# A two-layer graph attention network on one core: three pairs' attention, the second layer's bias additions and sums, and the last group's scaling put elsewhere in the order

## Chip, cores and metric

The kernel runs on one core of one Trainium2 chip. The metric is device time in microseconds (us) of one execution. TensorE (PE), VectorE (DVE), ScalarE (ACT), GpSimd (POOL) and SyncE (SP, which issues the DMAs here) each work through their instructions in the order in which the program lists them; waits between engines go by semaphores.

## The reference

128 graphs of 64 nodes with 768 features, fp32. Each of two layers is followed by a residual addition and a layer norm; x goes in, the output of the second norm comes out.

```python
# layer 0: gated graph attention, 12 heads of 64
h = einsum('bnd,ade->bane', x, W);  th = tanh(h)
attn = (th . w_src) + transpose(th . w_dst)
attn = softmax(where(~adj, -999, leaky_relu(attn, 0.2)))
f = elu(einsum('banm,bame->bane', attn, h) + b)       # heads side by side
gate = sigmoid(x @ H_w.T + H_b)
x = layernorm(x + gate * f + (1 - gate) * x)
# layer 1: masked self-attention, 6 heads of 128
q, k, v = x @ Wq + bq, x @ Wk + bk, x @ Wv + bv
p = softmax(q k^T / sqrt(128) + where(adj, 0, NEG))
x = layernorm(x + (p v) @ Wf + bf)
```

## The kernel before, in words

Two graphs make a tile of 128 rows; there are 64 tiles. `phase_a` (L304 to 773) does layer 0 and the value product of layer 1, for 32 pairs of tiles. `phase_b` (L776 to 1146) does the rest of layer 1 for 16 groups of two pairs.

*Dense products.* In phase A a product of a pair with a 768x768 matrix is done in a Strassen-like way with seven partial products instead of eight, each a step of three fp32 matmuls (`Product`, L196 to 250; the trace holds two matmul records for each, all at L208). It needs four sums of blocks of the transposed tokens, made on GpSimd by four instructions (`token_sums`, L254 to 260; "sums" below). The first partial product goes into a PSUM tile X; ScalarE copies it out (`snap`, L404), and the third partial product is added onto X, so the third cannot start before the first's snap is done. In phase B a similar scheme has R = 15 steps (`STEPS`, L37 to 53) that need 11 sums (`SUMS`, `SUM_STEPS`); those for F, the output product, are made on GpSimd by `pair_sum` (L842 to 846).

*The order.* Nothing schedules at run time or build time: each function is registered for a step in a table (`at`), and the steps are run through in order, functions of one step in the order of their registration (`run`, L262). With dense products as the clock of the table, this fixes every engine's queue. Pair p of phase A begins at o = 21 p: seven steps of W (h), seven of G (the gate), and seven of a value product V (`start_v`, L439 to 449). V belongs to an earlier pair: pair p's runs at o + 56, in pair p + 2. So pairs 0 and 1 have no V behind their G, nor has pair NP-2 = 30, whose seven steps are left free because pair 28's V was put into the last pair; the steps o + 14 to o + 20 of these three pairs hold no dense product.

*Attention of a tile in layer 0* (class `Tile0`, L455 to 623), with the steps that it has from its own start s (s = o for tile 1, which is first, o + 5 for tile 0, in the last pair o + 3): tanh of h; products with w_dst and w_src (`dst_mul`, `src_mul` on GpSimd, L467, L475) and their sums per head on VectorE (L470, L479); `dst_out` and `dst_in` send the dst scores to HBM and back, spread over the rows, as the tile s; `add` (L515, GpSimd adds src, then Prelu on ScalarE, L518); `mask` and `top` on VectorE (L522, L526); `exp`, twelve activations on ScalarE (L531); `scale`, a reciprocal and a multiplication on GpSimd for each half (L539, L541); `probs`, transposes on PE, copied by ScalarE (L552, L557); `aggregate` on PE (L570); `elu`, `mix1`, `mix2`; the layer norm, partly on GpSimd (`norm1`, L290 to 298: pow and shift) and with the normalisation on ScalarE (L302); `spill` to HBM. `gate_in` (L580, GpSimd) adds the gate's bias and `gate` (L584, ScalarE) takes its tanh.

For pairs 0 and 1 everything from `exp` on is two steps later for both tiles (`slow`), and tile 1's exps are kept in the table `late` and put at the end of their step, behind what the next pair registers there. The transposes of a pair's tokens and their sums stand at o - 6 to o - 4, for pairs 1, 2 and 31 by 7, 5 and 4 steps (`lead`) earlier.

*Phase B.* A group takes 90 steps: q and k for two halves, and in steps 60 to 89 the two F products (q = 0, 1 in the code) of the group before; the last group does its own F there. `load_x` fetches the residual rows, `add_bf` (L818 to 821) adds F's bias to them on GpSimd, two instructions for each q. The softmax of a group runs in tiles (q, i): in the last group maximum (`sm_top`), six exps on ScalarE (`sm_top_exp`, L952), and `sm_scale` (L968 to 971), a reciprocal on VectorE and one multiplication of 128x384 on GpSimd, then `probs` (L977, copied at L983) and `context` (L997).

The excerpt that shows how the order of the second F's sums is fixed before (f is the first step of that F):

```python
t = max(f - R + max(SUM_STEPS[: k + 1]) + 1, pr + 10)
at(t, lambda d=d, q=q, k=k: pair_sum(d, q, k))
```

Of the kernel before, what the change touches and what calls it, by code (L numbers as in the profile page):

```python
# [9 lines left out]
F32 = mybir.dt.float32  # L10
# [51 lines left out]
def kernel(  # L62
# [242 lines left out]
    def phase_a(ctx):  # L305
# [324 lines left out]
        late = {}  # L630

# [20 lines left out]
        for p in range(NP):  # L652
# [11 lines left out]
            if p:  # L664
                at(o - 20, lambda d=d: xb_in(d, 0))
                at(o - 16, lambda d=d: xb_in(d, 1))

                lead = {1: 7, 2: 5, NP - 1: 4}.get(p, 0)
                at(o - 6 - lead, lambda d=d: xT(d, 0))
                at(o - 5 - lead, lambda d=d: xT(d, 1))  # L670
                at(o - 4 - lead, lambda d=d: sums(d))
            else:
                at(0, lambda d=d: d.update(T=[transposed(t) for t in d["x"]]))
                at(0, lambda d=d: sums(d))
# [5 lines left out]


            slow = 2 if p < 2 else 0
            for i, s in ((1, o), (0, o + (5 if p < NP - 1 else 3))):
                t = Tile0(p, i)
                at(s + 6 + (i == 0), t.tanh, t.cap)
                at(s + 7, t.dst_mul)
                at(s + 8, t.src_mul)
                at(s + 9, t.dst_sum, t.dst_out, t.exchange)
                at(s + 10, t.src_sum)
                at(s + 13, t.dst_in)  # L690
                at(o + (14 if i else 16), t.gate_in)
# [12 lines left out]
                at(z + 24, t.probs)  # L704
                at(z + 25, t.aggregate)
                at(z + 26, t.elu)
                at(z + 27, t.mix1)
                at(z + 28, t.mix2)
                at(z + 29, t.norm1)
                at(z + 30, t.norm2)  # L710
                at(z + 31, t.spill)
# [58 lines left out]
        for step, fs in late.items():  # L770
            events.setdefault(step, []).extend(fs)
# [4 lines left out]
    def phase_b(ctx, wq, wk):  # L776
# [282 lines left out]
        for g in range(NG):  # L1059
# [35 lines left out]
            for q in range(2):  # L1095
                f = o + ((6 if last else 10) + q) * R
                for i in range(2):
# [88 lines left out]
```

## Time and profile before

| | us |
|---|---|
| median of three runs | 2965.62 |
| lowest, highest | 2964.14, 2966.01 |
| the profiled execution, as timed | 2965.09 |
| span of the profile | 2963.0 |
| VectorE busy | 1812.2 |
| GpSimd busy | 1642.1 |
| ScalarE busy | 1063.3 |

The profile is of one execution. Its page gives the busy time of each engine, the span in 40 slices, the chain of work that ended last and the costliest groups of instructions. Views of the trace list each engine's waits with what ended them, and its instructions in order of time; a line of such a timeline has start and length in us, the engine, the line of the code, the operation, output and inputs with shape, the number of instructions that the line stands for, and in brackets the idle time before and what ended it. Idle time matters on the engine that bounds the kernel, and there it is read stage by stage.

### The profile page before, as it was taken

The page shows a single profiled execution, that of the slowest core. Times are in us where ns is not written, and L with a number is a line of the kernel's source. Part 1 is how long each engine was busy: PE and PEld are TensorE (multiplying, and loading weights), DVE is VectorE, ACT ScalarE, POOL GpSimd, SP SyncE. Part 2 cuts the span into 40 slices and gives each one's busy share as a digit, 9 for nine tenths or more (in the row PEclk, how much of TensorE's full clock was granted, in tenths as well). Part 3 has the DMA queues.
Part 4 walks back from the last instruction along what each step waited for, and adds up shares of the span by engine and source line. Part 5 has one row for each costly group of instructions (what it writes and reads, how often), then busy time and mean ns, then how long its engine had stood idle before and what let it go on. Part 6 is the DMA issues. An engine that isn't in the chain of part 4 may idle for free.

```text
span 2963.0 us, 50040 instructions
## 1 busy us (share of the span) xinstructions
PE 2847.2 (96%) x18108; PEld 2063.0 (70%) x18108; DVE 1812.2 (61%) x3710; ACT 1063.3 (36%) x3011; POOL 1642.1 (55%) x1709
## 2 busy tenths in 40 slices
PE   7799999999999999999779999999999999999997
PEld 4455555555555555555448888888888888888886
DVE  4667667667677676676564555555555555555555
ACT  3354555545545545545432112222211222221222
POOL 3666666665665666665563544455454455455445
PEclk9899999999999999999899999999999999999999
DMA  6243443444544534534361112122212212211222
GB/s 183 84 143 114 133 146 113 144 132 123 148 122 133 148 114 133 149 114 136 112 197 40 56 64 87 55 86 87 74 56 76 87 55 87 87 66 62 78 81 70
DMA packets 358966, 309.13 MB, mean 104 GB/s; under 512 B 226625, under 2 KB 304193, under 8 KB 358721
## 3 DMA queue, kind: packets, MB, share of 16 engines
q1 hardware_dynamic: 358720, 305.95, 34.1%
q8 instruction: 144, 2.36, 0.3%
q14 instruction: 102, 0.83, 0.1%
HBM read 192.19 MB, written 101.06 MB: 99 GB/s over the span
## 4 chain that ended last, share of the span: by engine, by line
PE 60%; DVE 14%; POOL 10%; ACT 8%; DMA 5%; issue 3%; SPq 1%; POOLq 0%; DVEq 0%; ACTq 0%
PE X L863 42%; PE X L208 12%; ACT s L531 5%; POOL gt L580 3%; DMA xT_d<-T 2%; DVE s L522 2%; PE pb L997 2%; PE pb L928 2%; POOL s L541 2%; DVE nmx L526 1%; POOL th L475 1%; DVE pt L611 1%; DMA s<-dst_d 1%; DVE pt L602 1%; DVE pt L603 1%
## 5 line engine op out<-in xcount | busy, mean ns | idle before, releaser
L208 PE MATMUL X<-w,S 128*128 128x384 f32 x2304 | 804.1, 495 | 61.5 <-ACT snap L404 55.9
L208 PEld LDWEIGHTS X<-w,S 128*128 128x128 f32 x2304 | 431.8, 192 | 361.3 <-issue 59.0
L863 PE MATMUL X<-S,w 128*128 128x256 f32 x2816 | 668.0, 382 | 5.0 <-DVE q L889 2.4
L208 PE MATMUL X<-w,T 128*128 128x384 f32 x1728 | 598.5, 489 | 4.6 <-ACT snap L404 3.0
L863 PEld LDWEIGHTS X<-S,w 128*128 128x128 f32 x2816 | 523.2, 190 | 82.5 <-POOL shift L298 5.7
L208 PEld LDWEIGHTS X<-w,T 128*128 128x128 f32 x1728 | 327.9, 192 | 226.9 <-ACT snap L404 3.6
L845 POOL TENSOR_TENSOR Sc<-cT 128x256 f32<-128x256 f32 x224 | 160.8, 727 | 378.3 <-PE X L863 376.2
L863 PE MATMUL X<-w,Sc 128*128 128x256 f32 x1408 | 325.6, 383 | 1.9 <-DVE xs L906 1.9
L906 DVE TENSOR_TENSOR xs<-xs,X 128x256 f32<-128x256 f32 x512 | 208.5, 419 | 185.2 <-PE X L863 154.8
L863 PEld LDWEIGHTS X<-w,Sc 128*128 128x128 f32 x1408 | 264.5, 191 | 44.1 <-DVE xs L906 9.0
L531 ACT ACTIVATE s<-s,nmx 128x64 f32<-128x64 f32 x768 | 256.1, 336 | 93.3 <-DVE nmx L526 93.3
L889 DVE TENSOR_TENSOR k<-k,X 128x256 f32<-128x256 f32 x320 | 133.6, 421 | 217.8 <-PE X L863 167.9
L541 POOL TENSOR_TENSOR s<-s,rs 128x384 f32<-128x384 f32 x128 | 125.6, 981 | 220.4 <-DVE rs L539 156.0
L889 DVE TENSOR_TENSOR q<-q,X 128x256 f32<-128x256 f32 x320 | 132.2, 420 | 188.6 <-PE X L863 131.1
L863 PE MATMUL X<-xb,w 128*128 128x256 f32 x960 | 236.7, 379 | 0.0
L302 ACT ACTIVATE xs<-xs,shift,rstd 128x768 f32<-128x768 f32 x62 | 63.5, 1024 | 470.2 <-POOL shift L298 451.3
L404 ACT COPY snap<-X 128x384 f32<-128x384 f32 x288 | 136.1, 473 | 244.1 <-PE X L208 244.0
L467 POOL TENSOR_TENSOR tmp<-th,wd_bc 128x768 f32<-128x768 f32 x64 | 136.9, 2139 | 131.5 <-ACT th L463 131.5
L884 ACT ACTIVATE k<-X,bk_c 128x256 f32<-128x256 f32 x192 | 91.0, 474 | 305.2 <-PE X L863 305.2
L863 PEld LDWEIGHTS X<-xb,w 128*128 128x128 f32 x960 | 181.4, 190 | 23.8
L971 POOL TENSOR_TENSOR s<-s,rs 128x384 f32<-128x384 f32 x64 | 53.0, 828 | 227.6 <-DVE rs L970 204.7
L833 POOL TENSOR_TENSOR S<-xb 128x512 f32<-128x512 f32 x103 | 130.7, 1282 | 84.1 <-DMA xb<-xT_d 57.2
(109 smaller groups left out, 4072.9 us busy)
## 6 DMA issues: line engine op xcount, KB each, us to landing
xb<-in_x_dram SPq DMA_DIRECT2D x64, 384.0 KB
s<-dst_d SPq DMA_DIRECT2D x128, 192.0 KB
x_d<-xb SPq DMA_DIRECT2D x64, 384.0 KB
xT_d<-T SPq DMA_DIRECT2D x64, 384.0 KB
v_d<-v SPq DMA_DIRECT2D x128, 192.0 KB
xb<-xT_d SPq DMA_DIRECT2D x32, 768.0 KB
xb<-v_d SPq DMA_DIRECT2D x256, 96.0 KB
xs<-x_d SPq DMA_DIRECT2D x64, 384.0 KB
```

What stands on the lines that cost most here:

```text
L208: nc.tensor.matmul(o, self.lhsT(i, c), rhs, start=first and c == 0, stop=last and c == CH - 1, skip_group_check=True,)
L404: nc.scalar.copy(t, ps)
L467: nc.gpsimd.tensor_tensor(self.tmp, self.th, wd_bc, ALU.mult)
L531: nc.scalar.activation(self.s[:, a], self.s[:, a], AF.Exp, bias=self.nmx[:, a : a + 1], accum_out=self.sm[:, a : a + 1],)
L541: nc.gpsimd.tensor_tensor(t, t, rs[:, :, None].to_broadcast([P, A // 2, S]), ALU.mult)
L580: nc.gpsimd.tensor_tensor(self.g, self.g, hb_bc, ALU.add)
L833: eng.tensor_tensor(t, group_part(d, r0), group_part(d, r1), op)
L845: nc.gpsimd.tensor_tensor(t, pair_part(d, q, r0), pair_part(d, q, r1), op)
L863: nc.tensor.matmul(ps, self.lhsT(r, slot, c), self.rhs(r, slot, c), start=start and c == 0, stop=stop and c == 1, skip_group_check=True,)
L884: nc.scalar.activation(o[:, b], ps, AF.Identity, bias=bias[:, hd : hd + 1], scale=1.0 if positive else -1.0)
L889: nc.vector.tensor_tensor(o[:, b], o[:, b], ps, ALU.add if positive else ALU.subtract)
L906: nc.vector.tensor_tensor(o, o, ps, ALU.add if positive else ALU.subtract)
```

## The change

1. In phase A, for tile 1 of the pairs 0, 1 and 30: `dst_in` at s + 12 (was s + 13), `add` at s + 14 (was s + 17), mask and maximum at s + 15, exps at s + 16, scaling at s + 18 and s + 19. What follows from `probs` on is at s + 24 and on for all pairs; for pairs 0 and 1 it was two steps later, for both tiles. The table `late` is gone.
2. The token sums of pairs 1, 2 and 31 are at o - 4, as for the other pairs; the transposes keep their lead.
3. In the last pair tile 0 starts at o + 5 like in the others, its transposes for layer 1 are two steps later, and so are the pair's sums and its value product.
4. In phase B the second F's sums go each to one step behind its need (no longer behind all sums listed before it), or to that of the sums that it is made of; counted from f - R, the steps of the 11 sums go from 1, 2, 10, 10, 10, 10, 10, 10, 11, 12, 13 to 1, 2, 10, 10, 5, 9, 9, 8, 11, 12, 13. The bias additions are at f - 8 instead of f - 5, but for the last group.
5. In the last group the scaling is a reciprocal on VectorE and six activations on ScalarE of 128x64, each with its head's reciprocal as scale, in the place of one GpSimd multiplication; transposes and context are one step later, and so are F's sums.

```diff
-                lead = {1: 7, 2: 5, NP - 1: 4}.get(p, 0)
...
-                at(o - 4 - lead, lambda d=d: sums(d))
+                at(o - 4, lambda d=d: sums(d))
...
-            slow = 2 if p < 2 else 0
-            for i, s in ((1, o), (0, o + (5 if p < NP - 1 else 3))):
+            for i, s in ((1, o), (0, o + 5)):
...
-                at(s + 13, t.dst_in)
+                z = s - 3 if i and (p < 2 or p == NP - 2) else s
+                at(s + 12 if z < s else s + 13, t.dst_in)
+                at(z + 17, t.add)
                 at(o + (14 if i else 16), t.gate_in)
                 at(o + (16 if i else 18), t.gate)
-                at(s + 17, t.add)
-                at(s + 18, t.mask, t.top)
-                z = s + slow
-                if slow and i:
-                    late.setdefault(z + 19, []).extend((lambda t=t: t.exp(0), lambda t=t: t.exp(1)))
-                else:
-                    at(z + 19, lambda t=t: t.exp(0))
-                    at(z + (19 if i else 20), lambda t=t: t.exp(1))
+                at(z + 18, t.mask, t.top)
+                at(z + 19, lambda t=t: t.exp(0))
+                at(z + (19 if i else 20), lambda t=t: t.exp(1))
                 at(z + 21, lambda t=t: t.scale(0))
                 at(z + 22, lambda t=t: t.scale(1))
-                at(z + 24, t.probs)
+                at(s + 24, t.probs)
...
-                    at(o + 41 - i, lambda d=d, i=i: x1T(d, i, transposed(d["x"][i])))
+                    at(o + 43 - i, lambda d=d, i=i: x1T(d, i, transposed(d["x"][i])))
...
-                at(o + (47 if p < NP - 1 else 42), lambda d=d: x1_sums(d))
-            v = o + {NP - 4: 84, NP - 2: 50, NP - 1: 43}.get(p, 56)
+                at(o + (47 if p < NP - 1 else 44), lambda d=d: x1_sums(d))
+            v = o + {NP - 4: 84, NP - 2: 50, NP - 1: 45}.get(p, 56)
...
+        def sm_scale_act(d, q, i):
+            s, rs = sm_part(d, q, i), small.tile([P, HEADS], F32, name="rs1")
+            nc.vector.reciprocal(rs, d["sm", q, i])
+            for h in range(HEADS):
+                nc.scalar.activation(s[:, h], s[:, h], AF.Identity, scale=rs[:, h : h + 1])
...
-                        at(t + 5, lambda d=d, q=q, i=i: sm_scale(d, q, i))
-                        at(t + 7, lambda d=d, q=q, i=i: probs(d, q, i))
-                        at(t + 10, lambda d=d, q=q, i=i: context(d, q, i))
+                        at(t + 5, lambda d=d, q=q, i=i: sm_scale_act(d, q, i))
+                        at(t + 8, lambda d=d, q=q, i=i: probs(d, q, i))
+                        at(t + 11, lambda d=d, q=q, i=i: context(d, q, i))
...
-                pr = sm + (5 + 13 * q if last else 8 + 8 * q)
+                pr = sm + (6 + 13 * q if last else 8 + 8 * q)
+                ready = {}
...
-                        t = max(f - R + max(SUM_STEPS[: k + 1]) + 1, pr + 10)
+                        t = max(
+                            [f - R + SUM_STEPS[k] + 1, pr + 10]
+                            + [ready[r] for r in SUMS[k][:2] if r in ready]
+                        )
+                        ready[6 + k] = t
...
-                at(f - (1 if last else 5), lambda d=d, q=q: add_bf(d, q))
+                at(f - (1 if last else 8), lambda d=d, q=q: add_bf(d, q))
```

More of the change, by code (lines that the diff above doesn't have):

```diff
@@ L628, in at @@
             events.setdefault(max(step, 0), []).extend(fs)
-        late = {}
         def dense(d, key, i):
@@ L689, in phase_a @@
                 at(s + 10, t.src_sum)
-                at(s + 13, t.dst_in)
+                z = s - 3 if i and (p < 2 or p == NP - 2) else s
+                at(s + 12 if z < s else s + 13, t.dst_in)
+                at(z + 17, t.add)
                 at(o + (14 if i else 16), t.gate_in)
                 at(o + (16 if i else 18), t.gate)
-                at(s + 17, t.add)
-                at(s + 18, t.mask, t.top)
-                z = s + slow
-                if slow and i:
-                    late.setdefault(z + 19, []).extend((lambda t=t: t.exp(0), lambda t=t: t.exp(1)))
-                else:
-                    at(z + 19, lambda t=t: t.exp(0))
-                    at(z + (19 if i else 20), lambda t=t: t.exp(1))
+                at(z + 18, t.mask, t.top)
+                at(z + 19, lambda t=t: t.exp(0))
+                at(z + (19 if i else 20), lambda t=t: t.exp(1))
                 at(z + 21, lambda t=t: t.scale(0))
                 at(z + 22, lambda t=t: t.scale(1))
-                at(z + 24, t.probs)
[L705 to L711, printed above, removed]
+                at(s + 24, t.probs)
+                at(s + 25, t.aggregate)
+                at(s + 26, t.elu)
+                at(s + 27, t.mix1)
+                at(s + 28, t.mix2)
+                at(s + 29, t.norm1)
+                at(s + 30, t.norm2)
+                at(s + 31, t.spill)
             def x1_in(d, i):
@@ L769, in phase_a @@
         at(o + 30, lambda: load_T4(0))
-        for step, fs in late.items():
-            events.setdefault(step, []).extend(fs)
         run(events, N * NP + 60)
```

## The prediction

> **What bounds the kernel now.** The page comes first, for the engines' shares and the slices.
>
> ```profile
> PE 2847.2 (96%) x18108; PEld 2063.0 (70%) x18108; DVE 1812.2 (61%) x3710; ACT 1063.3 (36%) x3011; POOL 1642.1 (55%) x1709
> ...
> PE   7799999999999999999779999999999999999997
> ```
>
> TensorE (PE) is busy 96% of 2963.0 us: all that scheduling can win is its idle time, 2963.0 - 2847.2 = 115.8 us, plus matmuls that run slowly after a gap. The change removes no matmul. A slice is 74 us: the 7s are slices 1 and 2 (pairs 0 to 2), 20 and 21 (end of the first layer), and the last. Next, the waits of PE, for who ends its idle time (us in total, times, longest):
>
> ```profile
> PE X L208 <- ACT snap L404: 58.9, 33, 18.2
> PE pa L570 <- ACT pt L557: 10.0, 3, 7.3
> ...
> PE pb L977 <- POOL s L971: 6.8, 2, 6.1
> ```
>
> Half of it is one wait: the third product of a stage adds onto PSUM tile X, so it needs ScalarE's copy of X (the snap). The timeline of PE tells where (start, length, row, in brackets idle before and releaser):
>
> ```profile
> 59.50 8.72 PE L208 MATMUL X<-w,S 128*128 128x384 f32 x18 [6.90 <-ACT snap L404]
> ...
> 112.46 5.91 PE L208 MATMUL X<-w,S 128*128 128x384 f32 x12 [17.04 <-ACT snap L404]
> ...
> 1436.86 3.96 PE L208 MATMUL X<-w,S 128*128 128x384 f32 x6 [18.21 <-ACT snap L404]
> ...
> 1487.56 5.80 PE L208 MATMUL X<-w,S 128*128 128x384 f32 x12 [4.08 <-ACT snap L404]
> ...
> 2904.00 0.90 PE L977 MATMUL pb<-ident,s 128*128 128x128 f32 x3 [6.06 <-POOL s L971]
> ```
>
> So 42 us lie at three borders of pairs (0|1, 1|2, 30|31), just those where no value product follows the gate product. The snap itself takes 0.45; what delays it stands ahead of it on ScalarE. For 30|31 I followed that on GpSimd's timeline:
>
> ```profile
> 1418.72 1.80 POOL L475 TENSOR_TENSOR th<-th,ws_bc 128x768 f32<-128x768 f32 x1
> 1420.48 0.99 POOL L257 TENSOR_TENSOR S<-T 128x384 f32<-128x384 f32 x1
> ...
> 1423.45 0.99 POOL L260 TENSOR_TENSOR S<-T,S 128x384 f32<-128x384 f32 x1
> 1424.40 3.56 POOL L580 TENSOR_TENSOR gt<-gt,hb_bc 128x768 f32<-128x768 f32 x2
> 1427.91 1.47 POOL L515 TENSOR_TENSOR s<-s,src 128x768 f32<-128x768 f32 x1
> ```
>
> tile 0's source product, the next pair's four token sums, two gate additions, and only then tile 1's addition. Behind it follow Prelu 0.84, mask 0.96, maximum 0.95, twelve exps 4.0 (L531, 1432.27 to 1436.4), snap 0.45. From 300 to 400 us PE is 98.4% busy, from 1800 to 1900 99.9%: there is nearly nothing to win there.
>
> [...] over 112.5 to 116.5 the granted clock is 0.55 and 12 matmul records take 5.91 against 3.87 in the steady part; from 2904 to 2908 it is 0.50. A removed long gap is thus worth about 2 us more than itself. [...] The trace has 336 ns for L531. [...] L467 takes 1.8 alone and 2.14 on average. GpSimd times below may stretch by a fifth.
>
> **Part 1: tile 1's attention ahead in pairs 0, 1, 30; token sums at o-4.** Nothing is removed; the order on the engines changes. *Border 30|31.* The addition follows tile 0's source product directly, at 1420.48 instead of 1427.91: 7.43 earlier. Prelu, mask, maximum, exps and snap keep their lengths, but tile 0's gate tanh (0.83) now stands between exps and snap: 7.43 - 0.83 = 6.6. The sums now end near 1429.4, the first one needed (S[1]) near 1427.4, before PE resumes at about 1430.2, so the sums don't take the snap's place. PE stays cold after 11.5 us. **6.6 (5 to 7.5).** The DMA that fills tile 1's scores (dst_in, two issues on SP) goes one step earlier; it passes no transfer that PE awaits.
>
> *Border 0|1.* The exps (4.0) used to follow the next pair's first snap; they now precede it. Sums (3.9) leave GpSimd, but the addition waits for the dst DMA (issued 47.25, landing about 51.5): add to 53.0, Prelu 53.8, mask and maximum 55.8, exps 59.8, gate 60.6, snap 61.1. PE resumes near 61.2 instead of 59.50: **-1.7**. In return the exps no longer stand ahead of the later work of pair 1, whose matmuls then end near 94 instead of 95.41.
>
> *Border 1|2.* The norm's pow, now bound by VectorE near 94, then source product 1.8, a weight sum 1, the addition to about 99, and 0.84 + 0.96 + 0.95 + 4.0 + 0.83 + 0.45 = 8.0: PE resumes near 107.5 against 112.46. Tile 0's addition then stands behind two sums and scalings on GpSimd until about 114, so the fifth product starts near 116.2 against 119.32. Since probabilities to spill of pairs 0 and 1 come two steps earlier, pair 2 also loses its waits of 0.16, 0.78, 1.37 and 3.00 (157.92, a snap behind a normalise behind GpSimd) and that gap's cold matmuls (6.92 for two products instead of 3.87: 3.05). 3.1 + 0.16 + 0.78 + 1.37 + 3.00 + 3.05 = 11.5 at pair 3's start, border 0|1 within it; I take **11 (8 to 14)**, since these queues are replayed by hand.
>
> **Part 2: the last pair.** Tile 0's steps and the last value product go two steps later, so pair 28's first snap now stands ahead of tile 0's Prelu (which waited for its DMA to 1484.6): the 4.08 and its 1.9 of cold matmuls go. Pair 30's first two value products (3.9) come ahead of tile 0's transposes and aggregation and fill part of the 7.29 wait for L557; remaining waits: about 2 (probabilities), 1.4 (aggregation), 2.5 (tile 0's norm ahead of the last value product). 4.1 + 1.9 + 7.3 + 0.6 of small ones - 5.9 = **8 (4 to 11)**: two steps of delay cost up to 3.9 where nothing fills them.
>
> **Part 3: F's sums and bias additions in 14 middle groups.** The sums of the second F go to their own steps; the two additions of bf (L821, 3.58) move three steps ahead, past sums on GpSimd's queue.
>
> ```profile
> 2192.91 2.49 POOL L833 TENSOR_TENSOR S<-xb 128x512 f32<-128x512 f32 x2 [4.03 <-DMA xb<-xT_d]
> ...
> 2201.16 3.58 POOL L821 TENSOR_TENSOR xs<-xs,bf_bc 128x768 f32<-128x768 f32 x2
> ```
>
> They now wait for x (one burst with T4, ended 2194.3, stragglers 2195.1), and the sums k7, k5, k6, k2, k3 are queued behind them. Replayed: the fourth sum is ready 2202.5 to 2203.05, needed at 2203.3 for F's fourth step. Slack 0.2 to 0.8, with PE 99.9% busy: **-0.5 (-7 to +1.5)**, the low end 0.5 us in each of 14 groups.
>
> **Part 4: last group's scaling on ScalarE.** 4 GpSimd multiplications (0.83) go, 24 activations come.
>
> ```profile
> 2898.92 3.56 POOL L821 TENSOR_TENSOR xs<-xs,bf_bc 128x768 f32<-128x768 f32 x2
> 2902.44 0.72 POOL L845 TENSOR_TENSOR Sc<-Sc,cT 128x256 f32<-128x256 f32 x1
> 2903.12 0.83 POOL L971 TENSOR_TENSOR s<-s,rs 128x384 f32<-128x384 f32 x1
> ```
>
> The scaling stood behind bias additions and a sum until 2903.95. The trace shows no such activation: [...] at most 6 x 0.33 = 2.0. ScalarE has been idle from its first six exps (end 2895.0); scaling ends near 2899 even behind the second six, and the transposes come one step (0.86) later. Gone: 6.06 + about 1.9 cold (1.91 and 2.79 for what takes 1.03 and 1.89 warm) + 0.73, less a rest of up to 0.7: **8 (5.5 to 9.5)**. PE's wait of 1.9 at the end for a bias addition stays.
>
> **Sum.** 11 + 6.6 + 8 - 0.5 + 8 = 33.1. The profiled execution took 2965.09 by the clock of the runs (span 2963.0), the median of three is 2965.62: 2965.6 - 33 = **2932.6**.
>
> **Rivals.** *Half passed on (0.20):* what one wait loses the next takes: tile 0's addition and the third snap in pair 2 (all of border 1|2's 3.1 and half of pair 2's rest), tile 0's norm in pair 31. For it speaks that each border has several late things, against it that their queues were followed one by one. Parts 1 and 2 then give 6 + 3 for 11 + 8, part 3 costs 4, or 6 + 5.5 + 3 - 4 + 8 = 18.5: 2947 (2939 to 2953). *The moved order has no effect (0.03):* GpSimd's total work at a border is unchanged and still bounds it; then 2965 within 0.2%. Against: at 1427.91 the addition waits for GpSimd alone. *Slower (0.03):* the bias additions wait for x, and F's fourth sum behind them is late in each middle group; from x landing 0.8 us after the sums' end (2194.2 here) each further us costs 14. To overcome 33 it needs 2.4 beyond; 3 gives 42: 2965.6 - 33 + 42 = 2975. The burst's end at 2194.3 to 2195.1 speaks against it.
>
> **Numbers.** Forecast 0.74, rivals 0.20, 0.03, 0.03. The parts' bounds, taken as independent, give about ±9 round 2932.6; the top is stretched to the half-way case: 2924 to 2948 leaves out some 0.19. The runs of this kernel agree to about 0.1%; 0.2% (5.9 us) is what can be told from no change. Faster 0.95, same 0.02, slower 0.03.
>
> **What would show it.** PE's gaps: 6.9 grows to about 8.6; 17.0 becomes 12 to 14; 18.2 becomes 11.5; 3.00 (pair 2), 4.08 and 7.29 (last pair) vanish or shrink below 3; 6.06 becomes under 0.7. The first layer ends some 25 us earlier, the last group wins 8, and groups 2 to 14 keep their period of 87.3. I am wrong if that period grows, if snap waits of over 4 us appear elsewhere in pairs 1, 2 or 31, or if the exps still stand behind GpSimd's sums.

## The result, and the profile after

| | before | after |
|---|---|---|
| median of four runs, us | 2965.64 | 2933.49 |
| lowest, highest | 2964.14, 2966.01 | 2931.78, 2934.72 |
| span of the profile | 2963.0 | 2931.7 |

The ratio is 0.9892 (95% interval 0.9875 to 0.9909): 32 us less, within the forecast range and 0.9 us from the forecast. The terms of the forecast's sum were further off, and that is what the experiments are about.

The page of the changed kernel, the two lines shown of before (engines; PE's busy tenths in 40 slices):

```profile
PE 2840.5 (97%) x18108; PEld 2064.2 (70%) x18108; DVE 1809.9 (62%) x3710; ACT 1075.2 (37%) x3035; POOL 1643.0 (56%) x1705
...
PE   6899999999999999999889999999999999999998
```

The span fell by 31.3 and PE's busy time by 6.7, so 24.6 us of idle time went; the 6.7 are in the length of the matmuls' records, to be explained below. Its waits (us in total, times, longest):

```profile
PE X L208 <- ACT snap L404: 46.1, 34, 12.2
PE pa L552 <- POOL s L541: 12.9, 33, 2.9
...
PE pa L398 <- ACT xb L302: 3.8, 1, 3.8
...
PE pa L570 <- ACT pt L557: 1.2, 1, 1.2
```

The snap still leads, 12.8 us less; the wait for the last group's s (6.8) is gone from the list; the wait for pt fell from 10.0 to 1.2, but two new ones, for s at L541 (8.8 before) and for the normalised x of the last pair (L302), took over 7.9. The timeline of PE at the places of the prediction:

```profile
63.20 4.18 PE L208 MATMUL X<-w,S 128*128 128x384 f32 x6 [10.56 <-ACT snap L404]
...
109.17 4.06 PE L208 MATMUL X<-w,S 128*128 128x384 f32 x6 [12.03 <-ACT snap L404]
...
1421.27 4.18 PE L208 MATMUL X<-w,S 128*128 128x384 f32 x6 [12.22 <-ACT snap L404]
...
1488.11 0.55 PE L552 MATMUL pa<-ident,s 128*128 128x128 f32 x3 [2.89 <-POOL s L541]
...
1507.45 0.98 PE L398 MATMUL pa<-ident,xb 128*128 128x128 f32 x6 [3.76 <-ACT xb L302]
...
2912.69 2.86 PE L854 MATMUL X<-w,Sc 128*128 128x256 f32 x12 [0.77 <-DVE xs L897]
```

The gaps of the three borders are 10.6, 12.0 and 12.2 instead of 6.9, 17.0 and 18.2. Where the 31.3 us came from is read by lining up the same product in both timelines:

```
first product of              before    after   gained so far   in this stretch   forecast
pair 4                        209.42   199.62        9.8              9.8         11
pair 31                      1414.62  1405.01        9.6             -0.2          0
pair 31, third seven steps   1465.90  1451.40       14.5              4.9          6.6
second layer                 1542.43  1524.99       17.4              2.9          8
step 30 of group 2           1721.51  1706.05       15.5             -2.0          -
step 30 of group 15, the last 2855.24 2834.32       20.9              5.4         -0.5
end                          2963.01  2931.71       31.3             10.4          8
```

Five stretches gave less than forecast, two more. (Step 30 of a group begins q of its second half. The last group has 120 steps: F of the group before in steps 60 to 89, as in the others, and its own behind that, in 90 to 119; so from its step 30 on 90 steps are left.) Each column is one profile, and a few microseconds of such a difference can be chance: eight profiles of kernels with the changed order up to there have the start of pair 4 between 198.99 and 201.50. Lines of the second layer have other numbers in the changed kernel: L863 is L854, L906 is L897, L977 is L974, L971 is L968.

Three terms can be seen in the profile itself. *Border 30|31:* GpSimd and VectorE in the changed kernel:

```profile
1409.11 1.81 POOL L475 TENSOR_TENSOR th<-th,ws_bc 128x768 f32<-128x768 f32 x1
1410.88 1.47 POOL L515 TENSOR_TENSOR s<-s,src 128x768 f32<-128x768 f32 x1
1412.31 4.28 POOL L580 TENSOR_TENSOR gt<-gt,hb_bc 128x768 f32<-128x768 f32 x2
1416.55 0.99 POOL L257 TENSOR_TENSOR S<-T 128x384 f32<-128x384 f32 x1
```

```profile
1413.26 1.67 DVE L522 TENSOR_TENSOR s<-s,cap 128x768 f32<-128x768 f32 x1 [4.15 <-ACT s L518]
```

The order is the forecast one, the addition right behind the source product. But the mask now runs beside the gate additions and takes 1.67 instead of 0.96, while these take 4.28 for two instead of 3.56. The mask has 1.67 at all three borders, 0.7 us more on each path. So the gap is 12.2 and not 11.5. Then the clock: after 18.2 us of idle PE it was back at full rate 3.6 us after resuming (0.50 from 1436.9 to 1440.5), after 12.2 us only 5.8 later (0.50 from 1421.3 to 1427.1); half of the 2.2 is lost, 1.1. 18.2 - 12.2 - 1.1 = 4.9. The length of the gap alone does not decide that: of the eight profiles with this gap of 12.2, seven had 5.4 to 6.2 us of slow clock after it and one (u_sums_bf, an experiment below) 2.9. *Group 0:* the same three waits as before (0.84, 0.55, 2.36) at its start are followed by matmuls at a clock of 0.52 from 1532.8 to 1536.2, which before ran at 1.00: 1.7 us, though the order of work is the same. Of the fourteen kernels of this study, all with this order of group 0's products, ten took 1.5 to 1.7 us more there in their profile than the other four (the kernel before, u_border30, u_sums_bf and best1). The other 0.3 of the 2.0 lies in group 1 and belongs to the third part. *The middle groups* show theirs in the waits of the weight loads, in the experiment on the third part.

### The profile page after: what moved, and what is told of

The parts are those of the page before. It is cut to its first block, busy times and chain, and to the rows that moved or that the text cites. A ratio compares the mean times of both kernels' runs of the same rounds, so it can differ in the third digit from the quotient of the medians.

```text
span 2931.7 us, 50050 instructions
## 1 busy us (share of the span) xinstructions
PE 2840.5 (97%) x18108; PEld 2064.2 (70%) x18108; DVE 1809.9 (62%) x3710; ACT 1075.2 (37%) x3035; POOL 1643.0 (56%) x1705
## 3 DMA queue, kind: packets, MB, share of 16 engines
q8 instruction: 144, 2.36, 0.3%
## 4 chain that ended last, share of the span: by engine, by line
PE 58%; DVE 13%; POOL 11%; ACT 8%; DMA 5%; issue 3%; SPq 1%; POOLq 0%; DVEq 0%
PE X L854 41%; PE X L208 11%; ACT s L531 5%; POOL gt L580 3%; DMA xT_d<-T 2%; DVE s L522 2%; PE pb L994 2%; POOL s L541 2%; POOL th L475 2%; DVE nmx L526 2%; PE pb L919 2%; DMA s<-dst_d 1%; DVE pt L611 1%; POOL s L515 1%; DVE pt L602 1%
## 5 line engine op out<-in xcount | busy, mean ns | idle before, releaser
L854 PE MATMUL X<-S,w 128*128 128x256 f32 x2816 | 665.9, 382 | 3.7 <-DVE q L880 2.4
L854 PEld LDWEIGHTS X<-S,w 128*128 128x128 f32 x2816 | 525.4, 190 | 77.0 <-DVE q L880 2.8
L854 PE MATMUL X<-w,Sc 128*128 128x256 f32 x1408 | 322.7, 381 | 1.5 <-DVE xs L897 0.8
L897 DVE TENSOR_TENSOR xs<-xs,X 128x256 f32<-128x256 f32 x512 | 210.9, 420 | 170.4 <-PE X L854 161.2
L854 PEld LDWEIGHTS X<-w,Sc 128*128 128x128 f32 x1408 | 265.4, 190 | 39.8 <-POOL Sc L836 2.0
L531 ACT ACTIVATE s<-s,nmx 128x64 f32<-128x64 f32 x768 | 256.1, 335 | 94.0 <-DVE nmx L526 94.0
L541 POOL TENSOR_TENSOR s<-s,rs 128x384 f32<-128x384 f32 x128 | 128.2, 1003 | 210.0 <-DVE rs L539 140.8
L854 PE MATMUL X<-xb,w 128*128 128x256 f32 x960 | 236.6, 379 | 0.0
L302 ACT ACTIVATE xs<-xs,shift,rstd 128x768 f32<-128x768 f32 x62 | 63.5, 1025 | 418.9 <-POOL shift L298 372.4
L467 POOL TENSOR_TENSOR tmp<-th,wd_bc 128x768 f32<-128x768 f32 x64 | 138.6, 2166 | 133.0 <-ACT th L463 133.0
L854 PEld LDWEIGHTS X<-xb,w 128*128 128x128 f32 x960 | 181.2, 190 | 24.0
L875 ACT ACTIVATE q<-X,bq_c 128x256 f32<-128x256 f32 x192 | 91.1, 474 | 284.0 <-PE X L854 284.0
L968 POOL TENSOR_TENSOR s<-s,rs 128x384 f32<-128x384 f32 x60 | 49.7, 829 | 234.1 <-DVE rs L967 211.3
```

The lines of the kernel that those rows point to most:

```text
L302: nc.scalar.activation(r, r, AF.Identity, bias=shift, scale=rstd)
L467: nc.gpsimd.tensor_tensor(self.tmp, self.th, wd_bc, ALU.mult)
L531: nc.scalar.activation(self.s[:, a], self.s[:, a], AF.Exp, bias=self.nmx[:, a : a + 1], accum_out=self.sm[:, a : a + 1],)
L541: nc.gpsimd.tensor_tensor(t, t, rs[:, :, None].to_broadcast([P, A // 2, S]), ALU.mult)
L854: nc.tensor.matmul(ps, self.lhsT(r, slot, c), self.rhs(r, slot, c), start=start and c == 0, stop=stop and c == 1, skip_group_check=True,)
L875: nc.scalar.activation(o[:, b], ps, AF.Identity, bias=bias[:, hd : hd + 1], scale=1.0 if positive else -1.0)
```

## The experiments

Each of the first eight undoes something of the changed kernel; their cost is taken against its 2933.49. The four or five runs of a kernel lie 2 to 7 us apart, so a difference of 2 us is weak by itself and is read together with the trace. The parts are those of the prediction: part 1 is items 1 and 2 of the change, parts 2, 3 and 4 are its items 3, 4 and 5. In the code excerpts "..." stands for lines left out.

**Border 30|31 undone**

```diff
-                at(o - 4, lambda d=d: sums(d))
+                at(o - 4 - (4 if p == NP - 1 else 0), lambda d=d: sums(d))
...
-                z = s - 3 if i and (p < 2 or p == NP - 2) else s
+                z = s - 3 if i and (p < 2) else s
```

> The changed kernel with its first part undone for pair 30 alone (tile 1's attention at the old steps, pair 31's sums four steps earlier). By the prediction's sum this border is worth 6.6 us, so 2933.5 + 6.6 = 2940. The two traces say less: pair 31's first product gains on the old kernel from 9.6 us to 14.5 over this border, 4.9 in all, since PE stays at the lower clock longer after the shorter gap: then 2938.4, and PE's gap at the border is 18 us again with some 3.6 us of cold matmuls after it, instead of 12.2 and 5.9.

Measured 2937.24 (2935.30 to 2940.19), +3.75. The gap is back at 18.2, and the third seven steps of pair 31 come 4.6 us later than in the changed kernel, counted from pair 31's start. The smaller figure of the two traces holds, not 6.6; the reason that the expectation gives for it, a longer slow clock after the shorter gap, does not hold as a rule (2.9 in u_sums_bf after the same gap).

**Borders 0|1 and 1|2 undone** (pairs 0 and 1 with the old steps and the table `late`, sums of pairs 1 and 2 at o - 11 and o - 9)

```diff
-                at(o - 4, lambda d=d: sums(d))
+                at(o - 4 - {1: 7, 2: 5}.get(p, 0), lambda d=d: sums(d))
...
-                z = s - 3 if i and (p < 2 or p == NP - 2) else s
+                z = s - 3 if i and p == NP - 2 else s + 2 if p < 2 else s
...
```

> The first part undone for pairs 0 and 1 alone (old steps, tile 1's exps behind the next pair's first snap, everything from the exps on two steps later, sums of pairs 1 and 2 early again). The prediction gives 11: 2944.5. The two traces give 9.8 by pair 4: 2943.3. If what is lost there is caught up later in the first layer, it would be less than 5; the first layer has no slack between pairs 4 and 29 in the traces (both take 1128.5 us), so I expect the 10 to arrive whole.

Measured 2940.45 (2939.01 to 2941.20), +6.96; by the trace 8.5 us later at pair 4, and still 8.3 later at pair 31. It arrives whole, as expected, but is 2.7 (trace) to 4.0 us (runs) less than the forecast 11. Up to pair 4 this kernel has the order of the old one and yet is 1.3 us ahead of it there: so much the same order differs between two profiled runs. The two borders were not undone one by one.

**The last pair undone**

```diff
-            for i, s in ((1, o), (0, o + 5)):
+            for i, s in ((1, o), (0, o + (5 if p < NP - 1 else 3))):
...
-                    at(o + 43 - i, lambda d=d, i=i: x1T(d, i, transposed(d["x"][i])))
+                    at(o + 41 - i, lambda d=d, i=i: x1T(d, i, transposed(d["x"][i])))
...
-                at(o + (47 if p < NP - 1 else 44), lambda d=d: x1_sums(d))
+                at(o + (47 if p < NP - 1 else 42), lambda d=d: x1_sums(d))
...
-            v = o + {NP - 4: 84, NP - 2: 50, NP - 1: 45}.get(p, 56)
+            v = o + {NP - 4: 84, NP - 2: 50, NP - 1: 43}.get(p, 56)
```

> The second part undone (tile 0 of the last pair at o + 3, its transposes, sums and value product two steps earlier). The prediction gives 8: 2941.5. The two traces show only 2.9 between the start of pair 28's value product and the second layer: 2936.4. A rival: the shift of two steps is worth nothing or less, and the 2.9 come from the earlier border alone (then 2933.5 or below).

Measured 2935.57 (2933.52 to 2936.40), +2.08. By the trace the second layer begins 4.0 us later, counted from pair 31's third seven steps, and the end is 2.6 later: this profile has none of the late sums that cost the changed kernel's 1.6 us in the second layer (see the third part). Waits of 3.85 and 7.28 are back where they were, so the forecast was right about what goes; it was wrong about what comes. In the changed kernel PE waits in the last pair 0.90 and 2.89 for tile 0's scaled s and 3.76 for its normalised x, followed by slow matmuls (the clock is 0.50 from 1488.6 to 1492.0 and from 1509.0 to 1512.4). GpSimd shows what stands ahead of the scaling (tile 0's exps end at 1480.5):

```profile
1473.37 5.80 POOL L166 TENSOR_TENSOR w<-w 128x512 f32<-128x512 f32 x4
1479.13 0.99 POOL L257 TENSOR_TENSOR S<-T 128x384 f32<-128x384 f32 x1
...
1483.08 1.54 POOL L541 TENSOR_TENSOR s<-s,rs 128x384 f32<-128x384 f32 x1
1484.58 1.97 POOL L166 TENSOR_TENSOR w<-w 128x512 f32<-128x512 f32 x1
1486.52 1.54 POOL L541 TENSOR_TENSOR s<-s,rs 128x384 f32<-128x384 f32 x1
```

L166 makes sums of blocks of Wq for the second layer. They stand at fixed steps (o + 22 on); tile 0, two steps later, now comes behind two more of them and behind pair 30's token sums (L257 to 260).

**The third part undone, whole (u_sums_bf) and by halves** (the first of the two edits alone is u_sums, the second u_bf)

```diff
-                        t = max(
-                            [f - R + SUM_STEPS[k] + 1, pr + 10]
-                            + [ready[r] for r in SUMS[k][:2] if r in ready]
-                        )
+                        t = max(f - R + max(SUM_STEPS[: k + 1]) + 1, pr + 10)
...
-                at(f - (1 if last else 8), lambda d=d, q=q: add_bf(d, q))
+                at(f - (1 if last else 5), lambda d=d, q=q: add_bf(d, q))
```

> The third part undone (the second F's sums in the old order, bias additions at f - 5). The prediction took -0.5, so removing it should leave 2933.0. The two traces show groups of 86.74 us instead of 87.26 in most of the fourteen, 5.4 us in all: then 2938.9, with the four small stalls back in each group (steps 78 and 83 of one group, 9 and 10 of the next: 0.10, 0.07, 0.27, 0.07 us).

> Half of the third part undone: bias additions at f - 5 again, F's sums still spread. In the old order six sums (4.3 us) stood ahead of the two additions at f - 5 on GpSimd, in this one two (1.4). If the gain of the third part came from VectorE's accumulation getting its biased x earlier, the spread sums alone bring most of it: 2934 to 2935, no wait of VectorE for xs over 0.3 us. If it needs the three steps: 2937.8, as with both halves undone.

> The other half undone: F's sums in the old order, bias additions at f - 8. The additions are then ahead of all six sums and VectorE has its x early; the sums are done by about f, and F's fourth step needs the fourth sum at f + 3 (2.6 us later): 2933.5, nothing lost. It would also remove the small waits of F's fourth step for this sum in groups 1 and 4 of the changed kernel's trace. If instead the spread sums are what gained, 2937.8.

| | median (lowest to highest) | against 2933.49 | steps 30 of group 2 to 30 of group 15, profile |
|---|---|---|---|
| changed kernel | | | 1128.3 |
| both undone | 2937.80 (2936.98 to 2940.14) | +4.3 | 1133.7 |
| bias additions at f - 5, sums spread | 2930.20 (2928.26 to 2931.81) | -3.3 | 1127.6 |
| bias additions at f - 8, sums in old order | 2933.91 (2933.63 to 2936.08) | +0.4 | 1127.6 |

Counted from the start of group 1, up to which these kernels have the changed kernel's order, the three profiles end 7.4 later, 1.6 earlier and 0.2 later than its profile; what is left of each difference is not the third part's, since with the same order the start of group 1 itself came from 3.5 us earlier (both undone) to 2.2 later (sums in old order). Of the 3.3 that u_bf gained, the trace thus shows half.

Over these thirteen groups either half alone brings the time from 1133.7 to 1127.6, and both together no further (1128.3): they are two ways to the same thing. What it is, the old kernel shows on VectorE's timeline and in the waits of PEld, the weight loads (VectorE before; then PEld before, and PEld of the changed kernel; columns as in the fences of PE above):

```profile
2464.78 0.75 DVE L906 TENSOR_TENSOR xs<-xs,X 128x256 f32<-128x256 f32 x2 [1.49 <-POOL xs L821]
```

```profile
PEld X L863 <- DVE xs L906: 9.0, 30, 2.3
PEld X L863 <- POOL shift L298: 5.7, 12, 0.5
```

```profile
PEld X L854 <- POOL Sc L836: 2.0, 3, 1.0
PEld X L854 <- DVE xs L897: 1.6, 2, 1.2
```

With six sums ahead of them, the bias additions came so late that VectorE's accumulation into xs waited 1.49, F's fourth and ninth step with it (0.10 and 0.07). The tile norms behind that came late too; ScalarE's normalisation waited for GpSimd's shift (L298), and its copy of the next group's q out of PSUM (L884) stood behind that, which cost two steps of q 0.27 and 0.07: 0.52 in a group of 87.26, in twelve of the fourteen (0.18 in the other two). PE was 99.9% busy all the same, since these stalls lie inside the matmuls' records and left no gap: in the same place of q 24 records took 5.69 before and 5.34 in the changed kernel.

```profile
2481.83 5.69 PE L863 MATMUL X<-S,w 128*128 128x256 f32 x24
```

```profile
2463.04 5.34 PE L854 MATMUL X<-S,w 128*128 128x256 f32 x24
```

The new line, three waits for Sc, is the price that the prediction feared: with the bias additions three steps earlier a sum behind them is late in three of the groups (0.84 in group 1, 0.36 in groups 4 and 8). How often that happens differs from profile to profile: one to four times in five of the six profiles with spread sums and additions at f - 8, and never in the sixth (u_last). With the additions at f - 5 it happens in none of four profiles (u_bf and the three kernels at the end), and in u_bf every group takes 86.73 or 86.74.

**The fourth part undone, alone and with the third**

```diff
-                        at(t + 5, lambda d=d, q=q, i=i: sm_scale_act(d, q, i))
-                        at(t + 8, lambda d=d, q=q, i=i: probs(d, q, i))
-                        at(t + 11, lambda d=d, q=q, i=i: context(d, q, i))
+                        at(t + 5, lambda d=d, q=q, i=i: sm_scale(d, q, i))
+                        at(t + 7, lambda d=d, q=q, i=i: probs(d, q, i))
+                        at(t + 10, lambda d=d, q=q, i=i: context(d, q, i))
...
-                pr = sm + (6 + 13 * q if last else 8 + 8 * q)
+                pr = sm + (5 + 13 * q if last else 8 + 8 * q)
```

> The fourth part undone (last group's scaling on GpSimd, one step earlier). The prediction gives 8: 2941.5. The two traces show 10.4 between the last group's start and the end: 2943.9, with PE's wait of about 6 for s from GpSimd back, followed by cold matmuls. The four parts undone so far cost 3.8, 7.0, 2.1 and 4.3 = 17.1 of 32.2 us; if the parts simply add up this one would cost 15, and PE would have to lose 5 more than the two traces show there.

> Third and fourth part undone together. Alone they cost 4.3 and 4.7 us. If they are independent: 2933.5 + 9.0 = 2942.5. If both took away the same wait (bias additions and F's sums of group 14 standing ahead of the last group's scaling on GpSimd), both undone bring it back whole: steady groups 5.4 and last group 10.4 by the two traces, 2933.5 + 15.8 = 2949.3, with PE's wait for s of 6 us and cold matmuls after it.

Alone 2938.16 (2933.94 to 2941.17), +4.7: neither 8 nor 10.4. With the third part 2950.12 (2949.23 to 2951.74), +16.6, where the two alone sum to 9.0. Counted from the start of group 1 in the profiles, as above, it is 17.2, where the two alone sum to 7.4 + 4.0 = 11.4. PE's wait for s in the last group, alone and with the third part undone:

```profile
2878.34 0.55 PE L974 MATMUL pb<-ident,s 128*128 128x128 f32 x3 [1.89 <-POOL s L968]
```

```profile
2888.13 0.90 PE L974 MATMUL pb<-ident,s 128*128 128x128 f32 x3 [6.07 <-POOL s L968]
```

So the second theory of the joint run holds: F's sums and bias additions of group 14 were what stood ahead of the last group's scaling on GpSimd. Moving them away (part 3) takes 4.2 of the wait, moving the scaling away (part 4) all of it. From step 30 of the last group to the end the profiles show 108.9 with both undone, 101.5 with the scaling undone, 98.5 with sums and additions undone, 97.4 with neither. By the runs, then, the borders (3.75 and 6.96), the last pair (2.08) and parts 3 and 4 together (16.6) make 29.4 of the 32.2; the other 2.8 are no more than the scatter of these comparisons, and parts 1 and 2 were not undone together.

**Beyond the change: exps behind the next snap (e_late)**

```diff
...
-                at(o + (14 if i else 16), t.gate_in)
-                at(o + (16 if i else 18), t.gate)
+                fl = p < 2 or p == NP - 2
+                at(o + (23 if fl else 14 if i else 16), t.gate_in)
+                at(o + (24 if fl else 16 if i else 18), t.gate)
...
+                if z < s:
+                    late[o + 21] = [
+                        lambda t=t: t.exp(0), lambda t=t: t.scale(0), lambda t=t: t.exp(1), lambda t=t: t.scale(1)
+                    ]
...
```

> Beyond the change, for pairs 0, 1 and 30: tile 1's exps and scaling at the end of the next pair's first step, behind its first snap, and both gate additions and gate tanhs five steps and more later (o + 23, o + 24), behind the sums. At the border 30|31 the snap then waits for Prelu alone and the third product for GpSimd's second sum; by the lengths in the changed kernel's trace the sums would follow tile 1's addition directly (end 1412.3) and the second ends at 1414.4, so PE resumes near 1414.6 instead of 1421.27, but waits again for the scaled probabilities until about 1421 with one product done (3.9 cold). Net 3 to 4 us at each of three borders: 2923 (2921 to 2930). If what is left of the gap is passed on entirely to the probabilities' wait: 2933.

Measured 2928.75 (2925.12 to 2931.54), 4.7 less than the change, where about 10 were expected. The three gaps are 4.3, 6.7 and 6.1, now ended by GpSimd's second sum:

```profile
1412.17 4.21 PE L208 MATMUL X<-w,S 128*128 128x384 f32 x6 [6.09 <-POOL S L258]
```

17.7 us of gaps went, and 5.3 were gained by the start of the second layer: 2.9 at the first two borders and 2.4 at 30|31, not 3 to 4 at each. The rest was passed on: at 30|31, of 6.1 us less, 0.5 came back as a wait for s, 1.8 for pt and 1.3 for the third snap, since tile 1's chain of addition, mask, exps and scaling is as long as it was. At 1|2 a wait of 2.9 came that the trace puts down to a DMA.

**best1**, the same with bias additions at f - 5:

```diff
-                at(f - (1 if last else 8), lambda d=d, q=q: add_bf(d, q))
+                at(f - (1 if last else 5), lambda d=d, q=q: add_bf(d, q))
```

> The kernel with tile 1's exps and the gates behind the next pair's first snap (e_late), and bias additions at f - 5 with F's sums spread (u_bf). On their own the two gained 4.7 and 3.3 us on the changed kernel; they lie in different layers, so they should add up: 2925.5. If a part of each was the scatter of single runs (3 to 6 us between the highest and the lowest of four), 2927 to 2929.

Measured 2924.84 (2924.58 to 2928.01), ratio to before 0.9865 (0.9849 to 0.9880): the two add up, as expected, within the scatter (8.65 for 4.7 + 3.3). In the profiles it is 8.9 for 6.7 + 1.7, but 1.7 of the 8.9 come from group 0, where best1's profile alone of the three had no slow clock. This is the fastest kernel of the study; all its runs are below all runs of the changed kernel.

**best2**, the chain still further behind (`add` at the end of step o + 21, mask at o + 22, exps at the end of o + 23, the rest and tile 0 two steps later, the next pair's sums at o' - 9 and o' - 10), its core:

```diff
...
+                if fl and i:
+                    late[o + 21] = [t.add]
+                    at(o + 22, t.mask, t.top)
+                    late[o + 23] = [
+                        lambda t=t: t.exp(0), lambda t=t: t.scale(0), lambda t=t: t.exp(1), lambda t=t: t.scale(1)
+                    ]
...
-                at(o - 4, lambda d=d: sums(d))
+                at(o - {1: 10, 2: 9, NP - 1: 9}.get(p, 4), lambda d=d: sums(d))
```

> As best1, and for pairs 0, 1 and 30 the chain is moved further behind: sums of the next pair ahead of tile 0's source product on GpSimd (in its idle time of 5.6 us before the norm's pow), tile 1's addition and Prelu behind the next pair's first snap, exps behind its third, both tiles two steps later from then on. PE should then go on with three more products before it waits for tile 1's probabilities: the wait for the sums (4.3, 6.7 and 6.1 us in e_late) goes, and about 2 to 4 us of each border are left as a wait for s: 4 us less at two borders at least, 2917 (2913 to 2924). If the chain of tile 1 sets the end whatever stands before it, the whole gap reappears at the probabilities: 2925.

Measured 2949.60 (2946.50 to 2950.01): 25 worse than best1. The timeline of VectorE and of PE at border 30|31:

```profile
1426.87 1.25 DVE L383 STREAM_TRANSPOSE T<-xp 128x384 f32<-128x384 f32 x2 [5.87 <-DMA xp<-x_d]
1428.05 0.92 DVE L522 TENSOR_TENSOR s<-s,cap 128x768 f32<-128x768 f32 x1
```

```profile
1433.27 0.90 PE L552 MATMUL pa<-ident,s 128*128 128x128 f32 x3 [7.39 <-POOL s L541]
```

At step o + 22 stand the transposes of pair 29's tokens, which wait for a DMA; the mask, moved from o + 15 to o + 22, came behind them (its Prelu had ended at 1422.32, it began at 1428.05), and with it the whole chain. A new wait of VectorE of 5.9 took the place of the old one. Of the 25.4 us between the profiles of best2 and best1 this stretch of pair 31 accounts for 4.2; 11.2 were lost before pair 4. There, at border 1|2, it was another item: the next pair's sums on GpSimd and a mix on VectorE ran beside each other, and both took longer (three sums took 1.6 to 1.7 instead of 1.0, three instructions of the mix 1.6 to 2.4 instead of 0.9 to 1.0), the norm's pow came at 102.24 instead of 95.01 in the changed kernel, ScalarE's normalisation waited for that, and the first snap stood behind it: PE waited 9.79. What tile 0's two later steps add to that was not separated. The pairs behind also got their old waits of 3 us back (157.54: 3.01), from tile 0's two steps. The rest is 1.4 between pair 4 and border 30|31, 7.1 in the rest of the last pair, whose cause stays open, and 1.7 in group 0's clock.

**best3**, best1 with less ahead of tile 0's scaling in the last pair:

```diff
-                    at(z + 22, lambda t=t: t.scale(1))
+                    at(z + (21 if p == NP - 1 and not i else 22), lambda t=t: t.scale(1))
...
-                at(o + (47 if p < NP - 1 else 44), lambda d=d: x1_sums(d))
+                at(o + (48 if p == NP - 2 else 47 if p < NP - 1 else 44), lambda d=d: x1_sums(d))
...
-            at(o + 22 + k, lambda k=k: weight15_sum(early[0], k, nc.gpsimd))
+            at(o + (22 + k if k < 3 else 28 + (k - 3) // 2), lambda k=k: weight15_sum(early[0], k, nc.gpsimd))
```

> best1, and in the last pair nothing of other work ahead of tile 0's scaling: eleven of the fourteen sums of blocks of Wq (1.45 us each on GpSimd) and pair 30's token sums go behind it, and the second half's reciprocal on VectorE goes ahead of tile 1's mix. In the changed kernel tile 0's exps end at 1480.5, but the two halves are scaled only at 1484.6 and 1488.0, and PE waits 0.90 and 2.89 for them. If these queues are what the second part of the change left, both waits go: 3.8 us less, and the wait of 3.8 for tile 0's normalisation shrinks where it was part of the same chain: 2924.8 - 3.8 = 2921 (2918 to 2922). If the chain behind sets the end (tile 0's mix and norm up to the last value product), the 3.8 us reappear there and it stays at 2925.

Measured 2930.92 (2928.24 to 2932.37), 6 worse than best1; in the profiles 4.7 of it by the start of the second layer and 1.7 in group 0's clock. The waits of 0.90 and 2.89 are gone, which shows that these queues had caused them. But 3.29 came back at once as a wait for the copied probabilities:

```profile
1483.69 0.27 PE L570 MATMUL pa<-h,pt 64*64 64x64 f32 x1 [3.29 <-ACT pt L557]
```

ScalarE's copy waits for tile 1's mix on VectorE, which uses the tile pt as well (L612, ended at 1483.07), and so it did in best1, where it began at 1483.55 instead of 1483.16. These queues were thus worth 0.5 us at most. And the sums moved behind the scaling now stand ahead of the next thing of tile 0 on GpSimd, its norm's pow (VectorE's part of the norm ends at 1498.5):

```profile
1487.38 14.96 POOL L166 TENSOR_TENSOR w<-w 128x512 f32<-128x512 f32 x9
1502.30 0.99 POOL L295 TENSOR_TENSOR rstd<-rstd,neg_half 128x1 f32<-128x1 f32 x1
```

```profile
1505.38 1.55 PE L398 MATMUL pa<-ident,xb 128*128 128x128 f32 x6 [8.46 <-ACT xb L302]
```

3.8 us late there, and PE's wait for x grew from 3.8 to 8.5, 4.7 more. The nine took 1.66 each instead of 1.45, beside VectorE's own sums of that kind. A lighter spread was not tried.

## Why the prediction was right, and where it was not

The total was right to 1 us by luck, because errors of opposite sign met. Counted in the two profiles, parts 1 and 2 were put too high by 1.2 (borders of pairs 0 to 2), 1.7 (30|31) and 5.1, and 1.9 were lost in places that no term covers (0.2 between pairs 4 and 31, 1.7 in group 0); parts 3 and 4 were put too low by 5.7 and 2.4. 33.1 - 9.9 + 8.1 = 31.3. Of the signs that the prediction names, the first layer ended 17.4 us earlier and not 25, and the middle groups did not keep their period but shortened it, from 87.3 to 86.7.

- **What bounds the kernel**: right. 24.6 of 31.3 us are PE's idle time, and the gaps named are those that changed.
- **Part 1**: right mechanism, size too large. At 30|31 the term 6.6 measured 4.9 (3.8 in the runs): the mask's 0.96 was 1.67 and the clock came back 2.2 us later. The prediction said that GpSimd's times may stretch by a fifth, from L467's 2.14 on average for 1.8, but added nothing for VectorE's. At 0|1 PE resumed at 63.20, not 61.2: 1.3 of it because the dst scores landed that much later (addition at 52.80 instead of 51.5), 0.7 by the mask. At 1|2 it resumed at 109.17, not 107.5: 0.7 again by the mask, 1.0 because the norm's pow came at 95.0 and not near 94. At pair 3's start, where the prediction made its sum of 11.5, the gain was 10.9, again of two errors: up to the fifth product of pair 2 it was 1.3, not 3.1, and what went in the rest of pair 2 was 9.6, not 8.4. By pair 4 it was 9.8 (7.0 in the runs) for 11.
- **Part 2**: what was said to go did go: waits of 12.5 us were in this stretch before (4.1, 7.3, 0.4 and 0.7). The term of 5.9 for what remains was mis-sized: 0.3, 0.6, 0.9, 2.9, 3.8 and 0.2 are 8.7. And the 1.9 of slow matmuls didn't go: new slow stretches follow the waits of 2.9 and 3.8, and PE's busy time in this stretch rose by 0.8 (63.2 to 64.0). The step that failed is "remaining waits: about 2 (probabilities), 1.4 (aggregation), 2.5": other work on tile 0's path was not counted among what its later steps are moved past, on GpSimd the sums of Wq's blocks and pair 30's token sums, on ScalarE and VectorE tile 1's mix, which holds the tile pt.
- **Part 3**: "-0.5" was wrong, in sign too: 5.4 were gained over thirteen groups, 5.2 over all fourteen. The step that failed is "slack 0.2 to 0.8, with PE 99.9% busy": it looked for losses at the one sum and took a busy PE for a stage with nothing to win. The stalls of 0.52 a group were in the weight loads' waits. The loss it described does occur, in three of fourteen groups.
- **Part 4**: the last stretch gained 10.4, not 8: no rest of 0.7 was left, and the wait at the end, said to stay at 1.9, fell to 0.77 (it is 1.85 with the scaling undone and 1.88 with F's sums in the old order, so it takes both). Its six activations took 1.54 us: no trace had shown their length, and the author's estimate of at most 2.0 was six times one activation, of which the trace shows L531's 0.336 for the same 128x64. "About 1.9 cold" is 1.8 by its own figures (0.88 and 0.90). That parts 3 and 4 remove the same wait was overlooked; it did no harm to the sum, since the wait was counted once.
- **Rivals**: the half-passed-on case is what happened to part 2 (2.9 of 8), and to a smaller degree in part 1; for the whole kernel it was hidden by part 3. The slower case had its mechanism and place right, but not a price that decides.
- **The clock**: that a gap costs slow matmuls beyond itself is what the traces show: in the changed kernel the six records after the gap of 12.0 took 4.06 at a clock of 0.50, and six from 301.85 on, at 1.00, took 2.10. In the profiles before and after, every stretch at half clock is one to five times 3.41 us long, but for the last one of each, which the end cuts off (before 54.7 to 64.9, 99.0 to 116.1, 157.1 to 163.9, 1423.4 to 1440.5, 1488.3 to 1491.7, 1505.3 to 1512.1, 2901.4 to 2908.2 and from 2959.4; after 55.0 to 68.6, 99.3 to 113.0, 1413.5 to 1427.1, then 3.4 each from 1488.6, 1509.0 and 1532.9, and from 2929.0). Within each of the two all begin whole multiples of 3.41 us apart (from the first to the last 851 of them before, 842 after); counted from the span's start the first begins at 54.66 before and at 54.96 after. That what a gap costs beyond itself depends on where on this grid it falls is the author's estimate from these starts; it was not shown. After eight gaps of 12.2 us at 30|31 the slow clock lasted 2.9 to 6.2 us, after the two of 18.2 it lasted 3.1 and 3.6.

## What to carry to other kernels

When PE is nearly always busy, read the waits of the weight loads as well: the stalls of 0.52 us a group, which the matmuls' records covered, showed as waits only there, and half a microsecond in most of fourteen groups was 5 us. When something is moved in a hand-written order, list what stands at its new step on every engine that it uses, and what then stands ahead of the next thing that is waited for; best2 and best3 lost more than they won to such items. When a queue is cleared, ask what ends the wait next: best3 took 3.8 us of waits away and got 3.3 of them back from a tile still in use. Two edits that take away the same wait don't add, and undoing them one by one says too little of both; undo them together. Between two profiles 1.7 us of difference were the clock alone (group 0); compare the same stretch in all profiles that have its order.

## What was unexpected of the hardware

VectorE's mask of 128x768 took 1.67 us beside GpSimd's gate additions and 0.96 without, and of the two gate additions the first kept its 1.80 and the second took 2.53. In the changed kernel at 30|31 the mask began at 1413.26, in the middle of the first addition (1412.31 to 1414.11), and the second addition began at 1414.07, in the middle of the mask (to 1414.92). At border 1|2 the second was a weight sum, 1.72 instead of 0.99. In e_late the mask began at 1410.31, ahead of a token sum (1410.43), and kept its 0.96, while the sum took 1.69 instead of 0.99. In all of these whichever began first kept its length, and the one that began during it was about 0.7 us longer. Here, then, a mask that began just ahead of a GpSimd operation cost its own path nothing, and one that began 0.9 us into such an operation cost it 0.7.

That the slow clock came in whole steps of 3.41 us in the profiles before and after, beginning whole steps apart from one end of the execution to the other (54.7 to 2959.4, 55.0 to 2929.0), was not reckoned with either. It can make a profile's small differences a matter of chance: in group 0 the same three waits were followed by one such step in the changed kernel (1532.9 to 1536.3) and by none before (clock 1.00 from 1512.2 to 2901.3), and ten of fourteen profiles took 1.5 to 1.7 us more there than the other four. That the place of the waits on the grid decides it would fit, but was not shown.
